# A convolution regrouped from 96 + 96 to 128 + 64 channels, in a fused two-layer kernel

## The chip, the cores and the metric

The kernel runs on one core of a Trainium2 chip. The metric is the device time of one execution in microseconds (us). The core has a matrix engine (TensorE, PE), a vector engine (VectorE, DVE), a scalar engine (ScalarE, ACT), a general engine (GpSimd, POOL), and SyncE (SP), which here only issues DMA transfers. Each engine runs its own instructions in order and waits on semaphores where it needs another's result. A core has 128 partitions of on-chip memory (SBUF) and an accumulator memory (PSUM) that PE writes.

## The reference, cut to what matters

The input is `x` of shape (2, 96, 96, 96). Two layers follow each other, each a mixing block and a feed-forward block with quantized weights. Only the mixing block of layer 0 is touched:

```
xz = in_proj(layernorm(x));  xin, z = halves of xz (192 channels each);  z = silu(z)
t  = gelu(batchnorm(conv3x3(xin; 192 -> 192) + bias))
offset = tanh(conv1x1(t; 192 -> 2))                 # a shift of each position, in y and x
x_s    = grid_sample_bilinear(xin, position + offset)
# x_s is cut into 256 windows an image of 6 x 6 positions; four scan orders of each window:
dts, B, C = x_proj(x_s);  delta = softplus(dt_proj(dts) + bias)
h = h * exp(delta * A) + delta * x_s * B            # 192 channels x 16 states, 36 steps
y = sum over states of h * C, plus D * x_s;  the four orders are added
out = x + out_proj(layernorm(y) * z)
```

Layer 1 is an attention over cells of the image, a 5x5 depthwise convolution and another feed-forward block.

## The kernel before, in words

Layer 0 works in 32 stripes (2 images, 16 stripes of 6 rows and 96 columns: T = 576 positions, H2 = 288 half of it). A stripe has three parts.

The front (`_l0_front`) loads 8 rows of x (one above and one below the stripe), normalizes them, and projects to `xin` [96 partitions, 2 halves, 8 rows, 100 columns]: the 192 channels lie as two halves of 96, and each row has two columns of padding on either side. The convolution is 72 matmuls a stripe (`convolve`, line 567): for each output half (2) and each half of the rows (2), nine taps by two input halves, all of 96 x 96 x 288 columns in fp32, which the trace shows as two passes each. The tap is chosen by the offset at which `xin` is read. A gelu with the batch norm's scale and shift evicts each sum (line 578); two 1x1 convolutions whose weights are repeated over the columns give the offsets to every partition (line 596); POOL interpolates between neighbouring rows and columns (`sample`, lines 625 to 631); identity matmuls add the two terms (line 639), and ACT writes the windows in two orders, `xs0` and `xs1`. From these come B and C (line 676) and delta (lines 700, 740 to 762). The rows of C, delta and delta * x go to DRAM scratch (`c_d`, `dl_d`, `du_d`) and come back spread over partitions (`cre`, `dlr`, `dur`, lines 1036 and 1026).

The scan (`_l0_scan`, `_l0_section`) has 64 units a stripe. A unit: a matmul spreads B over the partitions (`bp`, line 1056), DVE multiplies it in place by `dur` (line 1060) and scans 128 x 864 elements (line 1076), with the decays `dA` from ACT (line 1041, three for two units); POOL multiplies by `cre` (line 1081) and PE sums the states into `y` (line 1093). There are two `bp` buffers, so the spread of a unit can run when the scan two units earlier has ended. The D term opens each `y` sum (lines 982 and 984).

The back (`_l0_back`, `_plan_ffn`) normalizes, gates, projects and runs the feed-forward block.

The order of all this is written by a planner (`_Plan`): every operation is given with an engine, an assumed cost and a due time; the planner plays the engines against each other and writes the instructions in the order of their planned starts. The front of stripe n + 1 and the back of stripe n - 1 are so woven into the units of stripe n on each engine, and on SP's queue. On the chip that order is fixed and each engine keeps to it, whatever the real times are. Ahead of the plan stands the setup (`_l0_weights`, `_ffn_weights`), whose loads go out on SP's and ACT's queues in the order of the code: `in_proj`, then the convolution weights `off1` (96 partitions x 13.5 KB), then the rest.

Of the kernel before, what the change touches and what calls it, by code (L numbers as in the profile page):

```python
# [9 lines left out]
F32 = mybir.dt.float32  # L10
# [88 lines left out]

SAME = 0.06  # L100
# [182 lines left out]
def _l0_weights(k, a, cp, tmp, ps, dram):  # L283
# [6 lines left out]

    k.w_in = load("in_proj", [C, 4 * C])
    k.w_c1 = load("off1", [C, 2, 9, 2 * C])
# [11 lines left out]
    bnv = tmp.tile([C, 5, 2], F32, tag="bnv", name="bnv")  # L304
    nc.sync.dma_start(bnv, a["bn"])
    k.bn_s = cp.tile([C, 2], F32, tag="bn_s", name="bn_s")
    k.bn_t = cp.tile([C, 2], F32, tag="bn_t", name="bn_t")
    nc.scalar.activation(k.bn_s, bnv[:, 4, :], AF.Sqrt, bias=k.eps5[:C])
    nc.vector.reciprocal(k.bn_s, k.bn_s)
    nc.vector.tensor_tensor(k.bn_s, k.bn_s, bnv[:, 1, :], ALU.mult)  # L310
    nc.vector.tensor_tensor(k.bn_t, bnv[:, 0, :], bnv[:, 3, :], ALU.subtract)
    nc.vector.tensor_tensor(k.bn_t, k.bn_t, k.bn_s, ALU.mult)
    nc.vector.tensor_tensor(k.bn_t, k.bn_t, bnv[:, 2, :], ALU.add)


    off2 = tmp.tile([C, 4], F32, tag="off2", name="off2")
    nc.sync.dma_start(off2, a["off2"])
    k.w_off = cp.tile([C, 4, C], F32, tag="w_off", name="w_off")
    nc.vector.tensor_copy(k.w_off, off2.unsqueeze(2).to_broadcast([C, 4, C]))
# [3 lines left out]
    xp = tmp.tile([C, 2, KG, 6 + 2 * NS], F32, tag="xp", name="xp")  # L323
    nc.sync.dma_start(xp, a["x_proj"])
    k.w_dl = cp.tile([C, 2, 2, C], F32, tag="w_dl", name="w_dl")
# [8 lines left out]
    k.w_bc = cp.tile([C, 2, 2, 4, 2, NS], F32, tag="w_bc", name="w_bc")  # L334
# [94 lines left out]
    ds4 = tmp.tile([C, KG, 2], F32, tag="ds4", name="ds4")  # L429
    nc.scalar.dma_start(ds4, a["Ds"])  # L430
    k.Dsum = cp.tile([C, 2], F32, tag="Dsum", name="Dsum")
    nc.vector.tensor_tensor(k.Dsum, ds4[:, 0], ds4[:, 1], ALU.add)
    nc.vector.tensor_tensor(k.Dsum, k.Dsum, ds4[:, 2], ALU.add)
    nc.vector.tensor_tensor(k.Dsum, k.Dsum, ds4[:, 3], ALU.add)
    k.w_D = cp.tile([C, 2, C], F32, tag="w_D", name="w_D")
    for half in range(2):
        nc.vector.tensor_scalar(
            k.w_D[:, half], k.ident[:C, :C], k.Dsum[:, half : half + 1], None, ALU.mult
        )
# [20 lines left out]
def _l0_front(k, P, S, f, x, b, s, at):  # L460
# [26 lines left out]
    xt, xin = temp([C, 8, HW], "xt"), S.tile(P.front, [C, 2, 8, HW + 4], "xin", 1)  # L487
# [39 lines left out]
    def project(half, c):  # L527
        pi = ps("pi")
        pe(N4, lambda: nc.tensor.matmul(
            pi.ap[:C, :N4], k.w_in[:, half * C : (half + 1) * C], xn.ap[:, 4 * c : 4 * c + 4, :],  # L530
            start=True, stop=True), ((xn, c),), (pi,), (xin,))
        act(N4, lambda: nc.scalar.copy(
            xin.ap[:, half, 4 * c : 4 * c + 4, 2 : HW + 2],
            pi.ap[:C, :N4].rearrange("p (r w) -> p r w", w=HW)), (pi,), ((xin, (half, c)),))
# [3 lines left out]
    for half in range(2):  # L538
        for c in range(2):
            project(half, c)  # L540

# [18 lines left out]
    t = temp([C, 2, T], "t")  # L560

    def convolve(oh, c):
        pc = ps("pc")

        def part(ih, tap):
            dy, dx = divmod(tap, 3)
            pe(H2, lambda: nc.tensor.matmul(  # L567
                pc.ap[:C, :H2],
                k.w_c1[:, ih, tap, oh * C : (oh + 1) * C],
                xin.ap[:, ih, 3 * c + dy : 3 * c + dy + 3, dx + 1 : dx + 1 + HW],  # L570
                start=(ih == 0 and tap == 0),
                stop=(ih == 1 and tap == 8),
            ), (xin,), (pc,), (t,))

        for ih in range(2):
            for tap in range(9):
                part(ih, tap)
        act(H2, lambda: nc.scalar.activation(
            t.ap[:, oh, c * H2 : (c + 1) * H2], pc.ap[:C, :H2], AF.Gelu,
            bias=k.bn_t[:, oh : oh + 1], scale=k.bn_s[:, oh : oh + 1]),  # L580
            (pc,), ((t, (oh, c)),), tab="g")

    for oh in range(2):
        for c in range(2):
            convolve(oh, c)
# [3 lines left out]
    fr = temp([C, 2, WIN, HW], "fr", 2)  # L589

    def offset(yx, c):
        po = ps("po")

        def run():
            for half in range(2):
                nc.tensor.matmul(
                    po.ap[:C, :H2], k.w_off[:, 2 * half + yx, :],
                    t.ap[:, half, c * H2 : (c + 1) * H2], start=(half == 0), stop=(half == 1))

        pe(2 * H2, run, ((t, (0, c)), (t, (1, c))), (po,), (fr,))  # L600

        def share():
            v = fr.ap[:, yx, 3 * c : 3 * c + 3].rearrange("p r w -> p (r w)")
            nc.scalar.activation(v, po.ap[:C, :H2], AF.Exp, scale=-2.0)
            nc.scalar.activation(v, v, AF.Ln, bias=k.one[:C])
            nc.scalar.activation(v, v, AF.Exp, scale=-1.0)

        act(H2, share, (po,), ((fr, yx),), tab="e", times=3)
# [5 lines left out]
    xs0 = f.xs0 = S.tile(P.hand, [C, 2, T], "xs0", 2)  # L614
    xs1 = S.tile(P.front, [C, 2, T], "xs1", 1)
    dif, top, bot = temp([C, 2, 7, HW], "dif"), temp([C, 2, WIN, HW], "top", 1), temp([C, 2, WIN, HW], "bot")
# [3 lines left out]
    def sample(half):  # L620
        v = lambda: xin.ap[:, half, 1:8, 2 : HW + 2]
        fy, fx = lambda: fr.ap[:, 0], lambda: fr.ap[:, 1]
        d, tp, bt = (lambda u=u: u.ap[:, half] for u in (dif, top, bot))
        D, TP, BT = (dif, half), (top, half), (bot, half)
        pool(672, lambda: tt(d(), xin.ap[:, half, 1:8, 3 : HW + 3], v(), ALU.subtract), (xin,), (D,))
        pool(T, lambda: tt(tp(), d()[:, 0:6], fx(), ALU.mult), (D, (fr, 1)), (TP,))
        pool(T, lambda: tt(tp(), tp(), v()[:, 0:6], ALU.add), (xin,), (TP,))
        pool(T, lambda: tt(bt(), d()[:, 1:7], fx(), ALU.mult), (D, (fr, 1)), (BT,))
        pool(T, lambda: tt(bt(), bt(), v()[:, 1:7], ALU.add), (xin,), (BT,))
# [3 lines left out]
        def add(c):  # L633
# [3 lines left out]
            def run():  # L637
                for n, u in enumerate((tp(), bt())):
                    nc.tensor.matmul(px.ap[:C, :H2], k.ident[:C, :C], u[:, rows, :],
                                     start=(n == 0), stop=(n == 1))  # L640

            pe(2 * H2, run, (TP, BT), (px,), (xs0, xs1))
            v = lambda: px.ap[:C, :H2].rearrange("p (i w j) -> p i w j", i=3, w=NW)
            act(H2, lambda: nc.scalar.copy(
                xs0.ap[:, half].rearrange("p (w i j) -> p i w j", w=NW, i=WIN)[:, rows], v()),
                (px,), ((xs0, (half, c)),))
            act(H2, lambda: nc.scalar.copy(
                xs1.ap[:, half].rearrange("p (w j i) -> p i w j", w=NW, j=WIN)[:, rows], v()),
# [13 lines left out]
    def order_of(o, xs):  # L662
# [4 lines left out]
        for c in range(2):  # L667


            def b_and_c(c=c):  # L670
# [3 lines left out]
                def run():  # L674
                    for half in range(2):
                        nc.tensor.matmul(
                            pb.ap[:, :H2], k.w_bc[:, half, o].rearrange("p j k n -> p (j k n)"),
                            xs.ap[:, half, cols], start=(half == 0), stop=(half == 1))
# [15 lines left out]
            def deltas(c=c):  # L694
# [3 lines left out]
                def run():  # L698
                    for half in range(2):
                        nc.tensor.matmul(  # L700
                            pd.ap[:C, :H2], k.w_dl[:, half, o, :], xs.ap[:, half, cols],
                            start=(half == 0), stop=(half == 1))
# [13 lines left out]
        block = lambda b: xs.ap[(b % NBL) * CB : (b % NBL) * CB + CB, b // NBL]  # L716
# [1250 lines left out]
```

## Time and profile before

| | us |
|---|---|
| median of 3 runs | 8392.63 (8389.98 to 8398.43) |
| profiled execution, in all | 8398.9 |
| its span, first to last instruction | 8397.1 |
| first scan on DVE starts at | 144.03 |
| busy in the span: PE / DVE / ACT / POOL | 7293.7 / 7812.2 / 6318.8 / 5177.2 |

Layer 0 runs to about 6380 us, layer 1 from there. In the views, a group's line gives: line of the kernel, engine, operation, output tile, input tiles, shapes and count, then busy time and mean nanoseconds of one, then the idle time of the engine just before them and what ended it. A line in order of time gives: start, duration, engine and the same names; in brackets the idle time before it. A line of waits gives: who waited, for whom, total us, number of waits, the longest. The name `off` stands for the convolution's weights in the rows of lines 288 and 567.

### The profile page before, as it was taken

What the parts mean: (1) busy time and instruction counts of PE and PEld (TensorE: products, weight loads), DVE (VectorE), ACT (ScalarE), POOL (GpSimd) and SP (SyncE); (2) the same over time, 40 slices, a digit from 0 to 9 for tenths busy, and PEclk for the clock granted to TensorE, in tenths of its full rate; (3) what the DMA queues carried; (4) which work ended last, traced back from release to release, by engine and by line L of the source; (5) the groups of instructions that cost most, each with busy time, mean ns of one, the idle gap of its engine ahead of it and who ended that gap; (6) DMA issues with size and microseconds to landing.
All of it is one profiled execution on the core that took longest, in us unless ns stands there. A gap on an engine that the chain in (4) does not pass through costs nothing. (4 is left out here: it accounts for less than half of the span.)

```text
span 8397.1 us, 118884 instructions
## 1 busy us (share of the span) xinstructions
PE 7293.7 (87%) x43653; PEld 3394.8 (40%) x43653; DVE 7812.2 (93%) x5398; ACT 6318.8 (75%) x10674; POOL 5177.2 (62%) x3835
## 2 busy tenths in 40 slices
PE   7888888888888888888888888888857999989998
PEld 4444444444444444444444444444423223542245
DVE  3999999999999999999999999999996998959988
ACT  5778777777777877777777777777745886778867
POOL 4888888788888888878788888888863000110001
PEclk8899998999889999989999889898857999989999
DMA  3444444444444454444444444444441000110001
GB/s 94 152 155 151 155 152 151 151 152 146 152 149 151 157 159 152 151 150 153 149 152 147 151 151 150 157 150 153 152 131 56 3 2 14 37 47 3 2 22 33
DMA packets 339992, 985.62 MB, mean 117 GB/s; under 512 B 50152, under 2 KB 51872, under 8 KB 339104
## 3 DMA queue, kind: packets, MB, share of 16 engines
q1 hardware_dynamic: 337488, 977.74, 37.0%
q8 instruction: 347, 5.69, 0.3%
q14 instruction: 253, 2.07, 0.1%
q10 hardware_dynamic: 1904, 0.12, 0.0%
HBM read 797.19 MB, written 139.25 MB: 112 GB/s over the span
## 5 line engine op out<-in xcount | busy, mean ns | idle before, releaser
L1081 POOL TENSOR_TENSOR h<-h,cre 128x864 f32<-128x864 f32 x2048 | 3497.2, 1714 | 1130.3 <-DVE h L1076 681.5
L1076 DVE TENSOR_TENSOR_SCAN h<-dA,bp 128x864 f32<-128x864 f32 x2048 | 3999.5, 1954 | 96.1 <-PE y L1093 19.1
L1041 ACT ACTIVATE dA<-dlr,A 128x576 f32<-128x576 f32 x3072 | 2156.1, 765 | 767.2 <-DVE h L1076 678.6
L1060 DVE TENSOR_TENSOR bp<-dur,bp 128x864 f32<-128x864 f32 x2048 | 2133.7, 1043 | 93.3 <-DMA dur<-du_d 39.6
L1093 PE MATMUL y<-h,fold 128*32 128x288 f32 (+2 forms) x18432 | 1847.4, 448 | 318.8 <-POOL h L1081 308.0
L567 PE MATMUL pc<-xin,off 96*96 96x288 f32 x4608 | 1334.6, 421 | 0.0
L1093 PEld LDWEIGHTS y<-h,fold 128*32 128x32 f32 x18432 | 761.3, 118 | 1085.4 <-POOL h L1081 579.9
L1056 PE MATMUL bp<-bt,selb 128*128 128x288 bf16 x2048 | 647.5, 317 | 534.1 <-DVE h L1076 512.7
L1429 ACT ACTIVATE pr<-sc 128x960 f32<-128x960 f32 (+1 forms) x1080 | 953.9, 937 | 200.8 <-PE sc L1425 178.6
L1509 DVE TENSOR_TENSOR sums<-sums,pr 128x3840 f32<-128x3840 f32 (+1 forms) x240 | 959.1, 3996 | 56.2 <-ACT pr L1429 34.2
L567 PEld LDWEIGHTS pc<-xin,off 96*96 96x96 f32 x4608 | 721.9, 167 | 410.2 <-issue 156.4
L1601 POOL MEMSET vch<- 96x32 f32 x16 | 2.4, 153 | 1301.7 <-DVE dist L1463 1208.4
L1056 PEld LDWEIGHTS <-selb 128*128 128x128 bf16 x2048 | 200.6, 98 | 1391.3 <-DVE h L1076 1125.1
L1425 PE MATMUL sc<-qH,kH 32*128 32x480 f32 (+1 forms) x3240 | 627.3, 602 | 10.2 <-DMA q<-qH 5.5
L1425 PE MATMUL sc<-q,kH 32*128 32x480 f32 (+1 forms) x1080 | 564.6, 602 | 0.0
L1491 PE MATMUL av<-pr,vT 128*32 128x480 f32 (+1 forms) x4320 | 533.7, 565 | 3.6 <-ACT av L1516 3.5
L1682 DVE SCALAR_TENSOR_TENSOR acc<-vch,lepe_w,acc 96x1152 f32<-96x1152 f32 x320 | 469.2, 1466 | 8.5 <-ACT vch L1617 0.8
L1425 PEld LDWEIGHTS sc<-qH,kH 32*128 32x128 f32 x3240 | 219.1, 184 | 419.8 <-issue 219.4
L883 POOL TENSOR_TENSOR x<-x,fy 96x576 f32<-96x576 f32 x32 | 55.6, 1738 | 478.7 <-ACT fy L882 414.7
L740 PE MATMUL pt<-xd,w_dt 96*128 96x288 f32 x768 | 299.3, 479 | 24.9 <-ACT r L746 11.9
L759 POOL TENSOR_TENSOR e<-e,du 128x576 f32<-128x576 f32 x192 | 231.1, 1204 | 50.5 <-ACT du L755 49.9
L745 ACT ACTIVATE e<-pt,dt_b 128x288 f32<-128x288 f32 x384 | 190.6, 496 | 93.6 <-PE pt L740 89.2
(270 smaller groups left out, 9858.7 us busy)
## 6 DMA issues: line engine op xcount, KB each, us to landing
cre<-c_d SPq DMA_DIRECT2D x1024, 288.0 KB
dur<-du_d SPq DMA_DIRECT2D x256, 864.0 KB
dlr<-dl_d SPq DMA_DIRECT2D x256, 864.0 KB
x<-xs SPq DMA_DIRECT2D x512, 72.0 KB
du_d<-du SPq DMA_DIRECT2D x128, 288.0 KB
dl_d<-dl SPq DMA_DIRECT2D x128, 288.0 KB
du_d<-du SPq DMA_DIRECT2D x128, 144.0 KB
dl_d<-dl SPq DMA_DIRECT2D x128, 144.0 KB
```

Of the source, the lines that this page charges most:

```text
L567: pe(H2, lambda: nc.tensor.matmul(pc.ap[:C, :H2], k.w_c1[:, ih, tap, oh * C : (oh + 1) * C], xin.ap[:, ih, 3 * c + dy : 3 * c + dy + 3, dx ...
L1041: nc.scalar.activation(dA.ap[:, :, blk, :], dlr.ap[:, blk, :].rearrange("p (c n) -> p c n", c=2), AF.Exp, scale=k.A[:, i, kg, h, blk : blk ...
L1056: nc.tensor.matmul(bp.ap[:, :H2], k.selb[:, kk, i, :], f.bc[o].ap[:, toks], start=True, stop=True)
L1060: nc.vector.tensor_tensor(bp.ap[:, : NBL * H2].rearrange("p (b n) -> p b n", b=NBL)[:, ::-1], dur.ap[:, ::-1, toks], bp.ap[:, :H2].unsquee ...
L1076: nc.vector.tensor_tensor_scan(hv, dv, bv, 0.0, ALU.mult, ALU.add)
L1081: nc.gpsimd.tensor_tensor(ht.ap, ht.ap, cre.ap[:, toks].unsqueeze(1).to_broadcast([128, NBL, H2]), ALU.mult)
L1093: nc.tensor.matmul(dst, k.fold, v, start=False, stop=stop)
L1425: nc.tensor.matmul(two[to // 2][:, to % 2, :n], kH[rows, k0 : k0 + 128], q, start=True, stop=True)
L1429: nc.scalar.activation(pr[:, 2 * i : 2 * i + 2, :n], two[i][:, :, :n], AF.Exp, scale=HD**-0.5)
L1491: nc.tensor.matmul((main if s < HEADS else other)[s * HD : (s + 1) * HD, :n], vT[:, blk, hd, :], pr[:, place(s, p), :n], start=at == 0, st ...
L1509: nc.vector.tensor_tensor(both, both, pr[:, :, :, :n], ALU.add)
L1682: S.op("dve", 1.43, lambda: nc.vector.scalar_tensor_tensor(acc.ap, src(), W.lw[:, t : t + 1], acc.ap, ALU.mult, ALU.add), (vch,), (acc,))
```

## The change

The 192 channels of `xin` are laid out as groups of 128 and of 64 (PART) instead of 96 and 96. Of the group of 64, a second copy is written to partitions 64 to 127, one column further on, by a DMA from SBUF to SBUF in every stripe; a matmul over these 128 partitions then does two neighbouring taps of that group. The outputs are grouped likewise: 128 output channels take 9 + 3 + 3 = 15 matmuls for each half of the rows; the other 64 take 15 pairs of matmuls, in which the two halves of the rows go to the lower and the upper 64 partitions of one PSUM tile and are evicted together. A stripe has 60 matmuls and 3 gelus instead of 72 and 4. Batch norm, offset, x_proj and D weights are laid out for the same groups, by three or four loads each instead of one (`parts`), and the D weights are cut by blocks of 32 channels. The convolution's weights are loaded by five DMAs that are operations of the plan, next to the first stripe's x, instead of one near the start. The unit, its tiles and the back are the same.

```diff
+PART = (128, 64)
...
+    def parts(dst, src, twice=False):
+
+        nc.sync.dma_start(dst[:C, 0], src[:, 0])
+        nc.sync.dma_start(dst[C:, 0], src[: 128 - C, 1])
+        for r in range(1 + twice):
+            nc.sync.dma_start(dst[64 * r : 64 * r + 64, 1], src[128 - C :, 1])
+
     k.w_in = load("in_proj", [C, 4 * C])
-    k.w_c1 = load("off1", [C, 2, 9, 2 * C])
+    k.w_ca = cp.tile([128, 9, 2 * C], F32, tag="w_ca", name="w_ca")
+    k.w_cb = cp.tile([128, 6, 2 * C], F32, tag="w_cb", name="w_cb")
...
+    S.op("sp", 1.0, lambda: nc.sync.dma_start(
+        xin.ap[64:, 1, :, 1 : HW + 1], xin.ap[:64, 1, :, 2 : HW + 2]),
+        ((xin, (1, 0)), (xin, (1, 1))), ((xin, "on"),))
...
-        for ih in range(2):
-            for tap in range(9):
-                part(ih, tap)
...
+    terms = [("a", dy, dx) for dy in range(3) for dx in range(3)]
+    terms += [("b", dy, None) for dy in range(3)] + [("b", dy, 2) for dy in range(3)]
...
+    def convolve(c):
+        pc = ps("pc")
+        for n in range(len(terms)):
+            def run(n=n):
+                w, v = term(slice(0, 128), c, n)
+                nc.tensor.matmul(pc.ap[:, :H2], w, v, start=n == 0, stop=n == len(terms) - 1)
+
+            pe(H2, run, reads(n), (pc,), (t,))
...
+    def convolve_rest():
+        pc = ps("pc")
+        for n in range(len(terms)):
+            def run(n=n):
+                for c in range(2):
+                    w, v = term(slice(128, 2 * C), c, n)
+                    nc.tensor.matmul(pc.ap[64 * c : 64 * c + 64, :H2], w, v,
+                                     start=n == 0, stop=n == len(terms) - 1)
+
+            S.op("pe", 0.6, run, reads(n), (pc,), also=(t,))
...
+        P.wa, P.wb = S.held(k.w_ca, "w_ca"), S.held(k.w_cb, "w_cb")
+        c1, split = a["off1"], 128 - C
+        taps = lambda v, dx: v.rearrange("c (y x) d -> c y x d", x=3)[:, :, dx]
+        for t, dst, src in (
+            (P.wa, k.w_ca[:C], c1[:, 0]), (P.wa, k.w_ca[C:], c1[:split, 1]),
+            (P.wb, k.w_cb[:64, 0:3], taps(c1[split:, 1], 0)),
+            (P.wb, k.w_cb[64:, 0:3], taps(c1[split:, 1], 1)),
+            (P.wb, k.w_cb[:64, 3:6], taps(c1[split:, 1], 2)),
+        ):
+            S.op("sp", 1.0, lambda dst=dst, src=src: nc.sync.dma_start(dst, src), (), (t,),
+                 due=-88 * tau)
         front(0)
```

## The prediction

> **What bounds the kernel now.** I read the page's busy line and its groups of instructions first, then a table of busy time by stretches of the span, then who VectorE (DVE) waited for, and last the first 150 us in order of time.
>
> ```profile
> PE 7293.7 (87%) x43653; PEld 3394.8 (40%) x43653; DVE 7812.2 (93%) x5398; ACT 6318.8 (75%) x10674; POOL 5177.2 (62%) x3835
> ...
> L1076 DVE TENSOR_TENSOR_SCAN h<-dA,bp 128x864 f32<-128x864 f32 x2048 | 3999.5, 1954 | 96.1 <-PE y L1093 19.1
> ...
> L1060 DVE TENSOR_TENSOR bp<-dur,bp 128x864 f32<-128x864 f32 x2048 | 2133.7, 1043 | 93.3 <-DMA dur<-du_d 39.6
> ...
> L567 PE MATMUL pc<-xin,off 96*96 96x288 f32 x4608 | 1334.6, 421 | 0.0
> ```
>
> The scan and its product are 3999.5 + 2133.7 = 6133 us of DVE, all in layer 0: 64 units a stripe of 3.0 us, 32 stripes. The convolution is the largest single item on TensorE (PE) after the y sums: 4608 passes (two for each of 72 matmuls a stripe), 1334.6 / 32 = 41.7 us a stripe. But PE is not the bound here:
>
> ```profile
> 6000.00:6340.00 340.00, 210.78 (x1377) 89.17 (x1371) 335.85 (x236) 187.07 (x320) 232.00 (x154) 0.64 0.42 133
> 200.00:6000.00 5800.00, 5002.59 (x29645) 2438.04 (x29648) 5659.13 (x4003) 4477.58 (x7762) 4729.41 (x3422) 0.91 0.48 151
> ```
>
> The columns after the length are busy PE, weight loads, DVE, ACT, POOL, then the granted clock. From 200 to 6000 us DVE is busy 97.6% of the time and PE 86%. In the last stripes, where no further front (and so no convolution) runs, PE falls to 62% at a clock of 0.64, and DVE rises to 98.8%. So removing the convolution wholly would gain about 1.2% of 5800 us, some 70 us, and halving it less. The same ceiling from the other side, DVE's waits between 200 and 6200 us:
>
> ```profile
> DVE bp L1060 <- PE bp L1056: 37.8, 38, 3.3
> DVE h L1076 <- PE y L1093: 19.1, 14, 2.2
> DVE bp L1060 <- POOL h L1081: 9.2, 7, 1.9
> DVE bp L1060 <- PE y L1093: 3.7, 4, 1.7
> ```
>
> PE keeps DVE waiting 37.8 + 19.1 + 3.7 = 60.6 us. The other place where layer 0 is not DVE-bound is its beginning: the first scan starts only at 144 us. In order of time:
>
> ```profile
> 1.21 0.41 SPq L288 DMA_DIRECT2D off<-in_off  x1
> 9.80 0.28 DVE L369 COPY w_dt<-dt_w 96x128 f32<-96x128 f32 x1 [6.90 <-DMA dt_w<-in_dt_w]
> 18.09 57.88 SPq L495 DMA_DIRECT2D xt<-in_x  x2
> 23.04 2.85 PE L506 MATMUL axc<-xt,less_mean 96*96 96x384 f32 x4 [0.39 <-ACT A L425]
> 36.48 35.22 PE L567 MATMUL pc<-xin,off 96*96 96x288 f32 x144
> 140.59 1.28 ACT L246 ACT_TABLE_LOAD   x1
> 141.89 4.10 ACT L1041 ACTIVATE dA<-dlr,A 128x576 f32<-128x576 f32 x6
> 144.03 3.80 DVE L1076 TENSOR_TENSOR_SCAN h<-dA,bp 128x864 f32<-128x864 f32 x2 [5.71 <-ACT dA L1041]
> 150.54 0.69 PE L1093 MATMUL y<-h,fold 128*32 128x288 f32 x6
> ```
>
> Small loads stay away until 9.8 us, behind the 1296 KB convolution weights issued at 1.21; the setup on DVE then runs to about 23 us, where the first matmul on x starts. The first stripe's convolution stands alone on PE for 35.2 us, with everything waiting; ACT is then nearly without a gap up to the first decay at 141.9.
>
> **The rule I weigh.** The Trainium skill, TensorEngine Tiling (Array Packing), Tiling Modes, says that a 128x64 setting gives two column tiles that load weights and multiply at the same time, and that a change of setting drains the array. The trace has no wide 64-column pair. Its nearest row is the y sum: three 32-column blocks, six passes, done in 0.69 us. One pass of the first convolution takes 35.22 / 144 = 0.245 us, so six in a row would be 1.47 us; three side by side are 2 x 0.245 plus some 0.2 to finish. The trace agrees for 32 columns, and I take it for 64; both ends are kept below.
>
> **The change, part by part.**
>
> 1. *Convolution of the first stripe.* Before: 72 matmuls x 0.489 us = 35.2. After: for 128 output channels 15 matmuls (9 taps of the 128-channel group, 3 double taps and 3 single taps of the 64-channel group) for each of two row halves, 30 x 0.489 = 14.7; for the other 64 outputs 15 pairs, 7.3 us if the two of a pair run side by side, 14.7 if not. Sum 22.0 or 29.3. I take 22.3 (a little for changes of setting): -12.9 us, all of it on the path. Ends: -13.2 and -5.9. The weights' last parts and the shifted copy hide: the copy is issued when the last eviction of xin is done (34.2 us), is first needed after nine matmuls of 0.489 (about 40.6), and a load four times its size, issued at 130.97, was in use at 136.28: 5.3 us at most.
>
> 2. *Setup.* The large load leaves the front of the queue, so the wait to 9.8 us shrinks; but batch norm, offset, x_proj and D now come in 14 loads instead of 4, all on SP (11 more there at 0.3 to 0.45 us an issue, +4.2 us; D leaves ACT's queue), and in the program's order the two largest weight pieces (some 800 KB) still stand ahead of x's first rows. The DVE part from x_proj's arrival to the first A (16.65 to 23.19) keeps its 6.5 us plus six w_D blocks instead of two (+0.8). SP's silence behind the large load, 1.62 to 9.89, is 8.3 us; less 4.2 for issues, 0.8 for w_D and about 0.8 for the pieces ahead of x, -2.5 us. Ends -5 and +1.
>
> 3. *An evicted convolution ahead of the first decay.* In the program's order, ACT's first gelu of the second stripe now comes before the first dA: one more table load and one gelu, 1.28 + 0.59 = +1.9 us, on the path, since ACT is busy without gaps there. Its matmuls will be done: 15 x 0.489 plus two dt matmuls from 132.5 ends at 141.5, as the table load does.
>
> Ramp: -12.9 - 2.5 + 1.9 = -13.5 us.
>
> 4. *Steady state, PE.* 144 passes a stripe become 60 plus 60 that share 30 slots: at the page's 0.29 us a pass, 41.7 us fall to 26.1 (34.8 if pairs don't overlap). None of that counts directly, only DVE's waits. The spread matmul that feeds each product sits in PE's queue behind whatever is ordered before it, with one unit, 3.0 us, to run in. Adding up the passes between neighbouring spreads in both programs' orders (0.245 us a 288-column fp32 pass, a third for the y sums), 63 of 2038 gaps hold over 3.0 us before, by 34.3 us together (near the measured 37.8); 22 do after, by 6.3 us. That is -28. I take -25, leaving 3 for new waits; ends -60 (all PE waits gone) and 0.
>
> 5. *Steady state, others.* ACT loses one gelu and some table loads a stripe (45 fewer loads in layer 0): 45 x 1.28 + 32 x 0.59 = 76 us of ACT, hidden, as ACT is at 77% here. POOL's samples have the same counts and columns, on 128 and 64 partitions instead of 96, and a 576-column operation takes 1.20 us at 96 (L626) and at 128 (L759) alike: nothing. D sums, projections and offset matmuls: same counts, nothing. Layer 1 is untouched.
>
> 6. *The new copy.* One 192 KB SBUF-to-SBUF load a stripe through SP. It adds a wait on ACT's eviction to SP's queue: behind it stand the C rows (cre), the decays' and products' inputs. And PE waits for it before its first double tap, with the spreads behind. In the order some four units (12 us) lie between the eviction's matmul and that tap. I cost it at nothing beyond those 3 us; without cover it is all DVE time (rival 3).
>
> Sum: -13.5 - 25 = -38.5. Profiled execution: 8397.1 span, 8398.9 in all, so 8360.4; the median of the three runs lies 6.3 us below the profiled one, so 8354.
>
> **Rivals.**
> 1. *Only the ramp is won.* DVE's waits come from bunching around the back's matmuls and from ACT's lag rather than from PE's load; the new order bunches elsewhere. For it: the waits come in a few places of a stripe, not spread out. Against: without fronts they vanish. -13.5: 8379, within 0.2%.
> 2. *The change doesn't do what it says: pairs run one after the other.* Ramp -6.5 (the first conv -5.9), gaps over 3.0 us sum to about what they were: 8386, no change. Against: the y row.
> 3. *Slower: the copy arrives late, and PE's queue stands on it.* SP's issues wait most of the time for POOL to give cre buffers back:
> ```profile
> SPq L1036 <- POOL h L1081: 2923.5, 822, 8.0
> ```
> 822 waits, the longest 8.0 us. A copy ordered behind such an issue goes out late by as much; the 864 KB loads next to it hold the DMA engines too. The slack is 12 us less 0.5 of eviction and up to 5 of load, 6.5 us; each us beyond it, in every stripe, costs 32 us. The gain is eaten at 38.5 / 32 = 1.2 us a stripe; at 2.7 us, +86 - 38: 8440.
>
> **How the numbers follow.** Forecast 0.58 (own range 8328 to 8374), rival 1 0.16, rival 2 0.07, rival 3 0.19. A measurement of this kernel can tell about 0.2%, 17 us: below 8376 is faster, above 8409 slower. Forecast and a sliver of rival 1 give faster 0.60; the rest of rivals 1 and 2, and the mildest late copies, same 0.22; slower 0.18. The range 8325 to 8418 leaves out about 0.06 below (all PE waits gone and setup at its best) and 0.13 above.
>
> **What would show it.** First convolution: about 22 us instead of 35.2 from its start (29 says rival 2). First matmul on x near 20.5 instead of 23.04. First scan near 130.5 instead of 144. DVE's waits on PE between 200 and 6200 us near 35 instead of 60.6; PE's busy share there near 78%. Wrong if PE's largest waits name the copy, if DVE's waits exceed 100 us, or if the first scan is not at least 8 us earlier.

## The result, and the profile after

| | us |
|---|---|
| median of 4 runs of the changed kernel | 8452.02 (8448.3 to 8454.08) |
| the kernel before, run beside it, median of 4 | 8395.53 (8389.98 to 8399.91) |
| ratio | 1.0063, 95% interval 1.0051 to 1.0075 |
| span of the profiled execution, before and after | 8397.1 and 8448.8 |
| first scan starts, before and after | 144.03 and 145.62 |
| last scan starts, before and after | 6342.84 and 6396.91 |

The change makes the kernel slower by 0.63%, some 53 us. The forecast was 8354, faster. From the first scan to the last it took 6198.8 us before and takes 6251.3 now: 52.5 us more, the whole loss. The ramp, where 13.5 us were to be won, is 1.6 us longer, and layer 1 is not touched.

First the page of the changed kernel (busy time of each engine, then groups: busy time and mean ns | idle time before them and what ended most of it):

```profile
PE 7291.4 (86%) x42885; PEld 3197.0 (38%) x42885; DVE 7824.0 (93%) x5404; ACT 6228.2 (74%) x10597; POOL 5167.7 (61%) x3835
...
L1117 DVE TENSOR_TENSOR_SCAN h<-dA,bp 128x864 f32<-128x864 f32 x2048 | 4000.5, 1953 | 76.8 <-ACT dA L1082 8.5
L1101 DVE TENSOR_TENSOR bp<-dur,bp 128x864 f32<-128x864 f32 x2048 | 2137.8, 1044 | 164.1 <-PE bp L1097 116.1
```

The scans and products cost what they cost before. DVE's idle time before the scans fell from 96.1 to 76.8 us and that before the products rose from 93.3 to 164.1: together 51.5 more, the loss again. PE's busy time did not fall: 7293.7 before, 7291.4 after. Next, the busy time between 200 and 6000 us of all work (the columns are PE, weight loads, DVE, ACT, POOL, the granted clock), and DVE's waits between 200 and 6300 us:

```profile
200.00:6000.00 5800.00, 4958.69 (x28704) 2234.86 (x28696) 5622.23 (x3969) 4357.74 (x7626) 4686.32 (x3396) 0.85 0.48 151
```
```profile
DVE bp L1101 <- PE bp L1097: 113.8, 178, 2.0
```

PE is busy for 44 us less than before (5002.6), where the forecast's 15.6 us a stripe made 468 in these 30 stripes. Its mean clock fell from 0.91 to 0.85. DVE waits for PE 178 times, 113.8 us in all, where it was 60.6; no wait names the copy.

The convolution itself did shrink: asked by its tile in that stretch, PE's time for it fell from 1260.6 to 803.7 us. The tiles below took more than half of that back, the rest of PE's work the remainder:

| PE busy 200 to 6000 us, by output tile | before | after | all at 128 rows (below) |
|---|---|---|---|
| pc, convolution | 1260.6 | 803.7 | 785.8 |
| po, offsets | 148.5 | 273.9 | 169.5 |
| pd and pb, delta, B and C | 373.0 | 424.0 | 368.5 |
| px, sum of the samples | 184.9 | 228.9 | 212.4 |
| y, sums over states and D | 1786.5 | 1822.4 | 1763.8 |

Not all of these rises have one cause. In a run below with fewer taps in the old layout, at a mean clock of 0.86, px takes 223.7 us and y 1852.4 as well, while po (147.7) and pd and pb together (380.6) stay near the old values. So the rise of px and y goes with the lower clock; that of the offsets, delta, B and C needs another reason.

The beginning of the changed kernel, in order of time:

```profile
19.86 0.43 SPq L507 DMA_DIRECT2D xt<-in_x  x1
...
23.03 2.84 PE L518 MATMUL axc<-xt,less_mean 96*96 96x384 f32 x4 [2.20 <-DMA xt<-in_x]
...
38.69 5.83 PE L601 MATMUL pc<-xin,w_ca 128*128 128x288 f32 x18
44.35 3.28 PE L601 MATMUL pc<-xin,w_cb 128*128 128x288 f32 x12
...
47.56 4.65 PE L601 MATMUL pc<-xin,w_ca 128*128 128x288 f32 x18
...
55.25 4.61 PE L614 MATMUL pc<-xin,w_ca 128*64 128x288 f32 x36
...
62.85 0.75 PE L635 MATMUL po<-t,w_off 128*128 128x288 f32 x2
63.62 0.75 PE L636 MATMUL po<-t,w_off 64*128 64x288 f32 x2
64.30 0.75 PE L635 MATMUL po<-t,w_off 128*128 128x288 f32 x2
64.98 0.75 PE L636 MATMUL po<-t,w_off 64*128 64x288 f32 x2
...
90.48 2.30 PE L741 MATMUL pd<-xs,w_dl 128*96 128x288 f32 x4
...
139.85 1.28 ACT L604 ACT_TABLE_LOAD   x1
141.58 0.59 ACT L604 ACTIVATE t<-pc,bn_t,bn_s 128x288 f32<-128x288 f32 x1 [0.44 <-PE pc L601]
...
143.48 4.10 ACT L1082 ACTIVATE dA<-dlr,A 128x576 f32<-128x576 f32 x6
145.62 3.80 DVE L1117 TENSOR_TENSOR_SCAN h<-dA,bp 128x864 f32<-128x864 f32 x2 [8.50 <-ACT dA L1082]
```

And the offset matmuls of the first stripe before:

```profile
71.54 4.04 PE L596 MATMUL po<-t,w_off 96*96 96x288 f32 x16
```

The convolution runs from 38.69 to about 62.85, 24.2 us instead of 35.2. The 36 passes at 55.25 are 9 pairs of 64-column matmuls, two passes each: 4.61 us in all, so the two of a pair do run side by side (18 slots of 0.245 make 4.4, 36 would make 8.8). But the eight offset matmuls that follow start 0.68 us apart; before, 16 passes of as many columns stood in 4.04 us, 0.505 a matmul. The first of each pair now reads 128 rows (partitions), the second 64, and at every alternation about 0.19 us is lost. The lead of 8.8 us when ACT takes up the first offset (64.87 against 73.64) is 2.7 us at the first softplus of delta (98.09 against 100.83) and gone by 126.8. The delta and B/C matmuls, which alternate in the same way, take 2.30 us for four passes at 90.48 where it was 1.21; part of that is a lower clock in that moment, for between 90 and 135 us the granted clock is 0.59 where it was 0.73.

The weight loads (PEld) show what happens at an alternation. Here are those of the convolution around 128, then 64, then 128 rows:

```profile
44.11 1.41 PEld L601 LDWEIGHTS pc<-xin,w_cb 128*128 128x128 f32 x6
45.90 1.27 PEld L601 LDWEIGHTS pc<-xin,w_cb 64*128 64x128 f32 x6 [0.39 <-issue]
47.55 4.19 PEld L601 LDWEIGHTS pc<-xin,w_ca 128*128 128x128 f32 x18 [0.39 <-issue]
```

Among rows of one number the loads follow one another, each beside the matmul pass before it. At each change of rows the load unit stands idle for 0.39 us: the next weights are loaded only when the pass before is nearly over (at 45.90, where the profile has that pass from 45.57 to 45.97).

In the steady state, a stretch of the changed kernel with two such pairs between two spreads; first PE, then DVE:

```profile
1072.81 1.33 PE L635 MATMUL po<-t,w_off 128*128 128x288 f32 x2
1074.07 1.33 PE L636 MATMUL po<-t,w_off 64*128 64x288 f32 x2
1075.33 1.33 PE L635 MATMUL po<-t,w_off 128*128 128x288 f32 x2
1076.58 1.32 PE L636 MATMUL po<-t,w_off 64*128 64x288 f32 x2
1077.84 0.42 PE L1097 MATMUL bp<-bt,selb 128*128 128x288 bf16 x1
```
```profile
1075.23 1.96 DVE L1117 TENSOR_TENSOR_SCAN h<-dA,bp 128x864 f32<-128x864 f32 x1
1078.47 1.06 DVE L1101 TENSOR_TENSOR bp<-dur,bp 128x864 f32<-128x864 f32 x1 [1.28 <-PE bp L1097]
```

Four offset matmuls hold PE for 5.03 us at half clock, 1.26 each (two passes at one setting take 0.96 at that clock). The spread behind them starts at 1077.84, when DVE's scan has ended at 1077.19, and the product waits 1.28 us. A unit lasts 3.0 us; what stands between two spreads must fit into it.

### The profile page after: what moved, and what is told of

It is laid out like the page before. It is cut to its first block, busy times and chain, and to the rows that moved or that the text cites. A ratio compares the mean times of both kernels' runs of the same rounds, so it can differ in the third digit from the quotient of the medians.

```text
span 8448.8 us, 117288 instructions
## 1 busy us (share of the span) xinstructions
PE 7291.4 (86%) x42885; PEld 3197.0 (38%) x42885; DVE 7824.0 (93%) x5404; ACT 6228.2 (74%) x10597; POOL 5167.7 (61%) x3835
## 5 line engine op out<-in xcount | busy, mean ns | idle before, releaser
L1117 DVE TENSOR_TENSOR_SCAN h<-dA,bp 128x864 f32<-128x864 f32 x2048 | 4000.5, 1953 | 76.8 <-ACT dA L1082 8.5
L1101 DVE TENSOR_TENSOR bp<-dur,bp 128x864 f32<-128x864 f32 x2048 | 2137.8, 1044 | 164.1 <-PE bp L1097 116.1
L1134 PE MATMUL y<-h,fold 128*32 128x288 f32 (+2 forms) x18432 | 1874.6, 451 | 398.8 <-POOL h L1122 380.0
L1097 PE MATMUL bp<-bt,selb 128*128 128x288 bf16 x2048 | 670.8, 328 | 453.2 <-DVE h L1117 438.4
L601 PE MATMUL pc<-xin,w_ca 128*128 128x288 f32 x1152 | 345.8, 421 | 0.0
L601 PEld LDWEIGHTS pc<-xin,w_ca 128*128 128x128 f32 x1152 | 202.3, 190 | 115.4 <-issue 66.9
```

What stands on the lines that cost most here:

```text
L601: nc.tensor.matmul(pc.ap[:, :H2], w, v, start=n == 0, stop=n == len(terms) - 1)
L1097: nc.tensor.matmul(bp.ap[:, :H2], k.selb[:, kk, i, :], f.bc[o].ap[:, toks], start=True, stop=True)
L1101: nc.vector.tensor_tensor(bp.ap[:, : NBL * H2].rearrange("p (b n) -> p b n", b=NBL)[:, ::-1], dur.ap[:, ::-1, toks], bp.ap[:, :H2].unsquee ...
L1117: nc.vector.tensor_tensor_scan(hv, dv, bv, 0.0, ALU.mult, ALU.add)
L1134: nc.tensor.matmul(dst, k.fold, v, start=False, stop=stop)
```

## The experiments

The theories named in the expectations are S: each change between matmuls of 128 and of 64 rows costs PE time; C: the lower granted clock is the cause; O: the new order bunches PE's work in other places; L: PE's queue stands on a late copy. The kernel before, run beside each of the three groups of runs on the same chip, took 8397.63, 8398.46 and 8400.53 us; the ratios below are to it.

### All at 128 rows, and the counter-test in the old layout

Every 64-row matmul that the change had made, and the single 64-column input projection, is widened to 128, with zero weights for the rows that don't belong. The places for the offsets, the single taps, and B and C; delta, the D sums and the sum of the samples are done likewise:

```diff
-                po.ap[:, :H2], k.w_off[rest, 1, yx], t.ap[rest, 2], start=False, stop=True)
+                po.ap[:, :H2], k.w_off[:, 1 + c, yx], t.ap[:, 2], start=False, stop=True)
...
-        return k.w_cb[:64, 3 + dy, m], xin.ap[:64, 1, rows, 3 : 3 + HW]
+        return k.w_cb[:, 3 + dy, m], xin.ap[:, 1, rows, 3 : 3 + HW]
...
-                            k.w_bc[: PART[half], half, o].rearrange("p j k n -> p (j k n)"),
-                            xs.ap[: PART[half], half, cols], start=(half == 0), stop=(half == 1))
+                            k.w_bc[:, half, o].rearrange("p j k n -> p (j k n)"),
+                            xs.ap[:, half, cols], start=(half == 0), stop=(half == 1))
```

> The changed kernel with every 64-row and single 64-column matmul widened to 128 rows and columns (zero weights in the added rows, outputs unchanged): the same matmuls in nearly the same order, without the changes between 64 and 128 rows; only the pairs of the last 64 outputs keep their 64 columns. Theory S (changes of row setting drain PE; in the changed kernel the offset's pairs take 0.68 us a matmul instead of 0.50 and a delta pair 1.23 instead of 1.04): PE busy falls by some 5 us a stripe, DVE's waits on PE fall from 114 us to 60 or less, time 8390 or less. Theory C (less PE work, so the granted clock falls, 0.85 instead of 0.91, and all PE work takes longer): the clock stays at 0.85 or lower, waits stay near 110, time within 10 us of 8452. Theory O (the planner's new order bunches PE work): waits stay near 110, 8452.

Measured: 8325.2 us (8319.12 to 8329.8), ratio 0.9916 (0.9899 to 0.9932). The same number of matmuls, more rows in them, and 127 us less than the changed kernel. Its busy times, DVE's waits and two of the offset matmuls:

```profile
200.00:6000.00 5800.00, 4646.15 (x29253) 2257.90 (x29244) 5721.40 (x4053) 4450.11 (x7797) 4781.02 (x3471) 0.90 0.50 155
```
```profile
DVE bp L1105 <- PE bp L1101: 15.0, 9, 3.2
```
```profile
61.42 0.65 PE L639 MATMUL po<-t,w_off 128*128 128x288 f32 x2
61.90 0.65 PE L640 MATMUL po<-t,w_off 128*128 128x288 f32 x2
```

The offset matmuls start 0.485 us apart instead of 0.68. PE is busy for 312 us less than in the changed kernel, DVE waits for it 15.0 us instead of 113.8, and the first scan starts at 135.82. This is what the regrouping is worth when the setting of rows stays the same. The order is not what changed: between 200 and 6300 us PE, DVE, ACT and POOL each run the same sequence of tiles in both kernels, without one difference. So theory O can't explain these 127 us.

The changes themselves can be counted in the traces (a change: a pass whose rows fall into another of the groups 65 to 128, 33 to 64, up to 32 than those of the pass before). Between 200 and 6000 us there are 468 in the kernel before, 1620 in the changed one and 457 here. At 0.195 us each, the price found further below, the 1163 that went are 227 us by estimate, most of the 312. The rest was not traced matmul by matmul; the clock, see the section on it, has a share.

The counter-test puts the alternation into the kernel before: the second matmul of each offset, B/C and delta pair reads 64 rows instead of 96 (32 channels are left out of these sums).

```diff
-                    po.ap[:C, :H2], k.w_off[:, 2 * half + yx, :],
-                    t.ap[:, half, c * H2 : (c + 1) * H2], start=(half == 0), stop=(half == 1))
+                    po.ap[:C, :H2], k.w_off[: 64 if half else C, 2 * half + yx, :],
+                    t.ap[: 64 if half else C, half, c * H2 : (c + 1) * H2], start=(half == 0), stop=(half == 1))
```

> The kernel before, in its own order, with the second matmul of each pair in the offset, B-and-C and delta projections on 64 rows instead of 96 (32 channels of the second half are left out there). Theory S: PE busy rises by 3 to 4 us a stripe, DVE's waits on PE rise from 61 to 90 or more, time 8425 to 8460. Theories C and O: the clock (0.91) and the order are those of before, waits near 61, time 8395 within 8.

Measured: 8416.69 (8402.84 to 8430.55), ratio 1.0020 (1.0011 to 1.0028): slower by 19 us with less work. The 16 offset passes of the first stripe take 5.22 us instead of 4.04, and DVE's waits on PE are 48.9 + 21.7 + 0.7 = 71.3 us. The sign is as S says, but time and waits stay below what S expected. The price of one change is nearly the same as in the changed kernel: 5.22 - 4.04 over the seven changes among these matmuls is 0.17 us. What differs is how much follows from it. There are 1166 changes between 200 and 6000 us, not 1620, and the offset tile takes 176.3 us, not 273.9, for the most part because its passes meet the full clock here and half of it in the changed kernel (table in the section on the clock).

### Which matmuls: the offset pair alone, and all but it

```diff
-                po.ap[:, :H2], k.w_off[rest, 1, yx], t.ap[rest, 2], start=False, stop=True)
+                po.ap[:, :H2], k.w_off[:, 1 + c, yx], t.ap[:, 2], start=False, stop=True)
```

> Changed kernel with only the second matmul of each offset pair widened from 64 to 128 rows (zero weights on the rows that are not its own), so this pair no longer alternates; the output is the same. Theory S (each alternation of 128- and 64-row matmuls costs PE time): the offset tile's PE time between 200 and 6000 us falls from 273.9 to about 170, about half of the PE time that all widenings together won, and the time falls from 8452 by a good half of the 127 us that they won: about 8385, waits on PE near 55. Theory O (bunching by order): unchanged, 8440 to 8452.

Measured: 8415.07 (8407.03 to 8426.8), ratio 1.0021 (1.0014 to 1.0028). The offset tile falls from 273.9 to 187.0 us, DVE's waits on PE to 72.9. The gain over the changed kernel is 37 us, less than the expected half of 127. The first scan stays at 145.63: in the ramp, POOL's interpolation covers the offset matmuls.

The complement leaves the offset pair alone and widens everything else.

> The complement: changed kernel with all the other 64-row matmuls (single taps, B and C rows, delta rows, D sums, identity sums, 64-column input projection) widened to 128 and only the offset pair left alternating; the output is the same. Theory S: what the other widening leaves, 8452 minus the rest of 127 us, about 8395 to 8415, offset tile near 274 us, waits on PE near 70. If only the offset pair mattered: 8440 to 8452.

Measured: 8375.34 (8367.99 to 8378.85), ratio 0.9970 (0.9957 to 0.9982). The offset tile stays at 275.7, waits on PE are 58.6, the first scan starts at 135.73. The gain is 77 us, more than expected; 10 of it is the ramp. The two parts, 37 and 77, nearly add up to the 127 of both.

```profile
DVE bp L1104 <- PE bp L1100: 72.9, 119, 1.8
```
```profile
DVE bp L1102 <- PE bp L1098: 58.6, 85, 2.4
```

The first line is DVE's largest wait with the offset pair widened, the second with all but it. I sorted DVE's waits on the spread by the tile that held most of PE, spreads and y sums aside, from 2.5 us before the wait to its end. In the changed kernel 35 us stand behind offset matmuls, 27 behind B/C and delta, 16 behind the next stripe's layernorm sum, 15 behind the output projection. With the offset pair widened the 35 are gone and the others stay; with all but it widened, 33 stay behind offsets, and of the B/C, delta and layernorm ones less than 1 is left. The waits behind offsets go with the offsets' alternation, most of the others with the rest of it.

### A change of setting, or the 64-row form itself

Widening takes away the 64-row form and the alternation at once. So first the alternation was increased with the same matmuls: the six terms of the 64-channel group stand double, single, double, single instead of three doubles, three singles.

```diff
-    terms += [("b", dy, None) for dy in range(3)] + [("b", dy, 2) for dy in range(3)]
+    terms += [("b", dy, dx) for dy in range(3) for dx in (None, 2)]
```

> Changed kernel with only the order of the last six terms of each convolution altered: double, single, double, single, double, single in place of three doubles and then three singles. The same matmuls and the same output; each chain has 4 more alternations of 128 and 64 rows, 12 a stripe. Theory S, by changes of setting (0.19 us a change at full clock, about 0.3 at half): the convolution's PE time between 200 and 6000 us rises from 803.7 by 70 to 110 us where the matmuls stand next to each other, less where others lie between; time 8460 to 8490. Theory S', that the 64-row form itself is the slow one whatever stands beside it: the convolution's PE time stays within 10 us of 803.7, time 8452 within 10.

Measured: 8463.35 (8454.25 to 8479.5), ratio 1.0075 (1.0058 to 1.0093). The same twelve passes in the first stripe, with all at 128 rows, in the changed kernel, and interleaved:

```profile
42.29 3.08 PE L606 MATMUL pc<-xin,w_cb 128*128 128x288 f32 x12
```
```profile
44.35 3.28 PE L601 MATMUL pc<-xin,w_cb 128*128 128x288 f32 x12
```
```profile
42.91 4.06 PE L601 MATMUL pc<-xin,w_cb 128*128 128x288 f32 x12
```

Four more changes cost 4.06 - 3.28 = 0.78 us, 0.195 each, at full clock; the three 64-row matmuls in a row cost 0.20 more than 128-row ones, about one change. So it is the change that costs, not the form. Between 200 and 6000 us the convolution's PE time rises from 803.7 to 844.5, less than the 70 to 110 for matmuls side by side, as other matmuls stand between: the traces count 222 more changes, so 0.18 us each.

The changed kernel's own trace says the same in all places. Taken over layer 0, at full clock and without idle time, the time from the start of one pass to the start of the second pass after it (all fp32 passes of 288 columns, the last two of one shape, the 64-column pairs left out) is:

| rows of the pass, then of the two after it | median us | found |
|---|---|---|
| 128, 128, 128 | 0.487 | 872 times |
| 64, 64, 64 | 0.488 | 154 |
| 128, 64, 64 | 0.682 | 277 |
| 64, 128, 128 | 0.679 | 100 |
| 128, 96, 96 | 0.488 | 43 |
| 96, 128, 128 | 0.490 | 85 |

A pass of 64 rows after one of 64 costs what one of 128 costs. A change between 128 and 64 costs 0.19 us either way, and one between 128 and 96 costs nothing: the old 96 + 96 layout met the 128-row matmuls of the units without loss.

The time of the interleaved run rose little. Its interval overlaps that of the changed kernel: DVE's waits on PE between 140 and 6400 us are 119.9 us against 116.1, so nearly all of those 41 us fall where PE has room.

Then it was to be decreased: every other offset pair is swapped, so that neighbouring pairs meet with the same rows.

```diff
-            nc.tensor.matmul(po.ap[:, :H2], k.w_off[:, 0, yx], t.ap[:, c], start=True, stop=False)
-            nc.tensor.matmul(
-                po.ap[:, :H2], k.w_off[rest, 1, yx], t.ap[rest, 2], start=False, stop=True)
+            two = [(k.w_off[:, 0, yx], t.ap[:, c]), (k.w_off[rest, 1, yx], t.ap[rest, 2])]
+            for n, (w, v) in enumerate(two[::-1] if c else two):
+                nc.tensor.matmul(po.ap[:, :H2], w, v, start=n == 0, stop=n == 1)
```

> Changed kernel with only the two matmuls of every other offset pair swapped (64 rows first, then 128), so that four neighbouring pairs hold 4 changes of row setting instead of 8; the same matmuls and the same output. By changes: the offset tile's PE time between 200 and 6000 us falls from 273.9 to some 210 to 240, as far as pairs stand next to each other, and the time from 8452 to about 8430. By the form itself: 273.9 within 5 and 8452 within 10.

Measured: 8460.08 (8455.11 to 8462.96), ratio 1.0067 (1.0050 to 1.0084). The PE part of the expectation nearly came (246.4 us for the offset tile, expected 210 to 240), the time did not: it is that of the changed kernel, and DVE's waits between 140 and 6400 us are 120.8 us against 116.1. The same stretch as above, in this kernel:

```profile
1072.43 4.80 PE L637 MATMUL po<-t,w_off 64*128 64x288 f32 x8
1077.17 0.42 PE L1097 MATMUL bp<-bt,selb 128*128 128x288 bf16 x1
```

The burst is 4.80 us instead of 5.03 and still far above a unit. It holds as many changes as before: between neighbours of 128 rows, 64, 128, 128, 64 makes four, and so does 128, 64, 128, 64. The four pairs stand side by side only in the first stripe; elsewhere units cut them apart, and over the stretch the swap left 1593 of 1620 changes. So this run did not do what its expectation supposed, and is no test of change against form. The offset tile gained by something else, the overlap told of in the last section. By the sorting above, waits behind offsets fell from 35 to 26 us, and those behind the output projection rose from 15 to 28, which nothing here explains. PE's busy time fell by 44 us without any gain: the sum of PE's work did not set DVE's waits here.

### The clock, with fewer taps in the old layout

The kernel before with 44 of its 72 convolution matmuls a stripe (7 taps of the second input half are left out):

```diff
-                stop=(ih == 1 and tap == 8),
+                stop=(ih == 1 and tap == 1),
...
-            for tap in range(9):
+            for tap in range(2 if ih else 9):
```

> The kernel before with 44 instead of 72 convolution matmuls a stripe, all 96 by 96 (seven taps of the second input half are left out): about the PE work of the changed kernel, without its row and column settings, copy and setup. Theory C: clock 0.85 to 0.86 between 200 and 6000 us, DVE's waits on PE over 90 us, and the ramp's gain of 13 us lost: 8430 to 8455. Theory S: the load is less and nothing drains, waits under 45, time 8350 to 8370. Theory O: between these, by its own new order.

Measured: 8328.23 (8324.22 to 8340.23), ratio 0.9916 (0.9899 to 0.9933).

```profile
200.00:6000.00 5800.00, 4769.29 (x28203) 2259.36 (x28202) 5708.12 (x4038) 4514.04 (x7855) 4765.76 (x3462) 0.86 0.49 153
```
```profile
DVE bp L1060 <- PE bp L1056: 22.9, 46, 2.1
```

The mean clock is 0.86, nearly the 0.85 of the changed kernel, yet DVE waits 22.9 us and the time falls by 69. A low mean clock alone is not the cause. But the mean hides something. In these traces the granted clock is at every moment either full or half, and what differs is which work meets the half. Read pass by pass over the offset tile, 200 to 6000 us:

| | mean clock in the stretch | offset passes at half clock | their mean clock |
|---|---|---|---|
| before | 0.91 | 10% | 0.95 |
| changed | 0.85 | 81% | 0.60 |
| all at 128 rows | 0.90 | 24% | 0.88 |
| offset pair alone at 128 | 0.86 | 40% | 0.81 |
| all but the offset pair at 128 | 0.88 | 81% | 0.59 |
| old layout, 64-row second matmuls | 0.90 | 10% | 0.95 |
| fewer taps | 0.86 | 8% | 0.96 |

One such burst in the changed kernel and the same one with all at 128 rows (PE, loads, DVE, ACT, POOL, then the clock):

```profile
670.20:682.80 12.60, 12.35 (x37) 4.89 (x36) 11.25 (x8) 12.02 (x21) 11.35 (x8) 0.50 0.41 133
```
```profile
651.30:659.20 7.90, 6.30 (x37) 3.34 (x36) 7.80 (x6) 7.74 (x13) 7.61 (x5) 1.00 0.35 84
```

So in the changed kernel the offsets pay twice: for the changes, and for the half clock that most of them meet. Of the 104 us between 273.9 and 169.5, about half is the price of the changes by estimate (240 matmuls, 0.195 us at full clock, 0.30 at half, in the shares of the widened kernel), the rest the clock. The run with fewer taps does not test this, since its offsets meet the full clock. Widening the offset pair alone, with the order untouched, halves their share at half clock, so the alternation has a part in it; what sets the clock, the runs don't show.

The run also shows the forecast's main idea alone: fewer convolution passes, no new layout, no copy, and DVE's waits fall from 60.6 to 22.9 us.

### The copy

The copy is left out, and the double taps read the first group in its place (part of the sum is left out). Its operation is also gone from the plan, which moves the order.

```diff
-    S.op("sp", 1.0, lambda: nc.sync.dma_start(
-        xin.ap[64:, 1, :, 1 : HW + 1], xin.ap[:64, 1, :, 2 : HW + 2]),
-        ((xin, (1, 0)), (xin, (1, 1))), ((xin, "on"),))
...
-            return k.w_cb[:, dy, m], xin.ap[:, 1, rows, 1 : 1 + HW]
+            return k.w_cb[:, dy, m], xin.ap[:, 0, rows, 1 : 1 + HW]
```

> The changed kernel without the copy of the 64-channel group (the double taps read the 128-channel group in its place; that part of the sum is left out). If the copy were late and PE stood on it (theory L), waits fall below 60 and the time to 8400 or less. Theories S and C: waits and time as in the changed kernel, 8440 to 8455.

Measured: 8405.87 (8395.29 to 8413.58), ratio 1.0009 (1.0000 to 1.0018), waits on PE 70.5 us: 46 us less than the changed kernel, which none of the theories had expected in this size. That could be a late copy or the other order. So the copy was put back, the order with it, and only the reading was changed:

```diff
-            return k.w_cb[:, dy, m], xin.ap[:, 1, rows, 1 : 1 + HW]
+            return k.w_cb[:, dy, m], xin.ap[:, 0, rows, 1 : 1 + HW]
```

> Changed kernel, same planned order, the copy still made, but the double taps read the first channel group in place of the shifted copy's group, so no matmul waits for the copy (part of the sum is left out). The run without any copy had won 46 us (8405.9), but its planned order had moved too. Theory L (PE's queue stands on a late copy): the same gain here, about 8405, VectorE's waits on PE between 200 and 6300 us near 70 instead of 113.8. Theory O (the gain of the run without a copy came from its other order) and theory S (the changes of row setting are the whole cause): 8450 within 15 us, waits near 114.

Measured: 8460.07 (8449.95 to 8471.57), ratio 1.0075 (1.0058 to 1.0092).

```profile
DVE bp L1101 <- PE bp L1097: 111.6, 176, 1.9
```

No gain: PE never stood on the copy to any effect, and L falls. The 46 us came with the other order, or with the absence of the transfer as such; these two were not told apart. The traces favour the order: without the copy's operation all four engines run another sequence than the changed kernel, and 36% of the offset passes meet half clock, not 81%; with the copy unread the sequence is that of the changed kernel, and the share is 84%. So O is not excluded as an amplifier, since where the alternating bursts fall decides how much of them DVE feels. As the cause of the 127 us it is excluded by the widenings, which leave the sequence as it is.

### x's place in SyncE's queue

All matmuls at 128 rows, and x's first load is no longer ordered behind the zeroing of its border row, with the convolution's weights due later:

```diff
-        pool(8, lambda: nc.gpsimd.memset(xt.ap[:, 0, :], 0.0), (), (xt,))
+        pool(8, lambda: nc.gpsimd.memset(xt.ap[:, 0, :], 0.0), (), ((xt, "edge"),))
...
-        (xt,),
+        ((xt, "body"),),
...
-                 due=-88 * tau)
+                 due=-80 * tau)
```

> All widened to 128 rows as in the run that took 8325.2, and x's first load no longer ordered behind the padding memset, with the convolution weights planned later, so that x is issued earlier than at 19.9 us. If the setup term of the forecast was lost to the place of x's load in SyncE's queue: x's first matmul near 20.5 instead of 23.0, first scan near 133 instead of 135.8, time 8322. If the set-up on VectorE holds it: 23.0 as before, 8325.

Measured: 8320.94 (8315.0 to 8326.19), ratio 0.9905 (0.9889 to 0.9922). The difference to 8325.2 is within what can be told apart, but the ramp shows it plainly:

```profile
16.30 0.60 SPq L512 DMA_DIRECT2D xt<-in_x  x1
...
20.96 2.85 PE L523 MATMUL axc<-xt,less_mean 96*96 96x384 f32 x4 [0.39 <-ACT A L440]
...
132.01 3.80 DVE L1121 TENSOR_TENSOR_SCAN h<-dA,bp 128x864 f32<-128x864 f32 x2 [5.86 <-ACT dA L1086]
```

x goes out at 16.30 instead of 19.58, its first matmul starts at 20.96 instead of 22.84, and now waits for the set-up of A as in the kernel before. The first scan comes at 132.0. This kernel is the fastest here, 0.95% below the kernel before and 131 us below the changed one.

## Why the prediction was wrong

**Part 5 is the step that failed.** It set the largest term at nothing. It said of D sums, projections and offset matmuls "same counts, nothing". The counts are the same; the rows are not, and each change from 128 to 64 rows and back costs. The second matmul of each of these pairs has 64 rows now, so every pair brings two changes. The passage I weighed ahead of the change (the Trainium skill, TensorEngine Tiling (Array Packing), Tiling Modes) says that a change of the tiling mode drains the array. I used its half on parallel column tiles and gave its other half "a little", for the convolution alone. The runs put a size on it: 0.195 us a change in the interleaved convolution, 0.68 against 0.485 us a matmul in the offsets, and some 1150 changes more than before between 200 and 6000 us, 225 us of PE time by estimate. The half clock in the offset bursts came on top; no part of the prediction had a term for it. Taking all of the alternation away, in the same order of work, returns 127 us.

**Part 4 was right in its mechanism and failed through part 5.** I took PE's waits down from 60.6 to 35; they rose to 113.8. The arithmetic over the gaps between spreads used one price for a pass, that of the full clock and without changes, so it could not see that the bursts of pairs had grown beyond a unit. With 128 rows everywhere the waits are 15.0, below my figure and inside the ends that I gave; with fewer taps in the old layout 22.9. Less convolution does free DVE, by more than I counted.

**Part 1** held: pairs overlap, and the convolution took 24.2 us where I said 22.3 (ends 22.0 and 29.3); 1.2 of the 1.9 is half clock at its start (its first 18 passes took 5.83 us, the next such 18 took 4.65). The steady state agrees: 803.7 us in the 5800 for 30 stripes' worth of passes (3600 of 120 a stripe) are 26.8 a stripe, against the 26.1 forecast. Its gain of 11 us then did not reach the first scan: at 126.8 us the lead was nearly zero, because the delta and B/C pairs stand on the ramp's path as well. Widening everything but the offsets brings the first scan to 135.73; there the clock between 90 and 135 us is 0.81, not 0.59, so the clock may have a part in this gain too.

**Part 2**, setup, was -2.5 and came out as 0. x's first load was issued at 19.86, not earlier but 1.8 us later than before, behind two weight pieces and k, v and q's weights. The 14 small loads took 0.63 us each on SyncE's queue, 3.04 to 11.86, where I had counted 0.3 to 0.45, and SyncE then stood 2.5 us at q's weights until the first weight piece had landed. x's first matmul waited 2.20 us for it and started at 23.03 (before 23.04). The set-up had become shorter as forecast, ACT's part of A ending at 21.1. With x's load moved ahead the 2.1 us appear.

**Part 3**, +1.9 for a table load and a gelu ahead of the first decay, is there to the line: 139.85, 141.58, then the decays at 143.48.

**Part 6** held: the copy cost nothing that could be shown. Of the rivals, the one that was slower named the wrong place, the copy. The "only the ramp is won" rival supposed that the waits come from bunching, not from the sum of PE's load. That is closer to what happened, though the ramp was not won, and the bunches were lengthened by the alternation and the half clock, not moved by the order.

The sum by its terms, ramp and steady state: forecast -13.5 and -25; measured +1.6 and +52.5.

## What to carry to other kernels

Where a contraction of 192 rows is cut into 128 + 64, pad the 64 with zero weights to 128 unless many 64-row matmuls follow one another: here more rows made the kernel 127 us faster. Groups of 96 and 128 rows met without loss. A matmul's price depends on its neighbour in PE's order, so count the changes of row setting as well as the passes, above all in bursts that must fit between two deadlines. When a part gets cheaper and PE's busy time does not fall, ask for PE's time by tile: the tile that was not meant to change shows the cost. Ask for the clock in that tile's own bursts, too: a mean over the stretch, 0.85 against 0.86 here, can hide that one tile gets half of it.

## What the runs showed that was not expected

- A change between 128 and 64 rows in fp32 passes of 288 columns costs 0.195 us at full clock, nearly a pass of 0.245, while a change between 128 and 96 costs nothing. At half clock an offset matmul took 1.26 us.
- 64-row matmuls on the lower and then the upper 64 partitions, next to each other, overlap. With every other pair swapped, the trace has the passes of the two starting within 0.01 us of each other (63.358 and 63.365), and the first stripe's offset passes, with four changes among them, take 4.05 us, no more than 16 passes at one setting (4.04 before the change):

```profile
62.60 4.05 PE L637 MATMUL po<-t,w_off 128*128 128x288 f32 x16
```

- The granted clock follows neither PE's busy time nor its matmuls in a simple way: between 200 and 6000 us 0.91 at 5002.6 us busy (before), 0.85 at 4958.7 (changed), 0.90 at 4646.2 (all at 128 rows), 0.86 at 4769.3 (fewer taps). The changed kernel and the widened one run the same matmuls in number and order, and the one with more rows has the higher clock, most of all in the offset bursts. How much of the 127 us goes through the clock could not be separated, since the clock can't be set.
